# Moving one weight load in SyncE's queue: the gates' input weights behind the second group's first rows

## The chip, the cores and the metric

The kernel runs on one core of a Trainium2 chip. The metric is the device time of one execution in microseconds; the kernel before has a median of 2111.39 us over 7 runs (2110.67 to 2114.44). A core has TensorE (PE in the profile), VectorE (DVE), ScalarE (ACT), GpSimd (POOL) and SyncE (SP), each with its own list of instructions, and 16 DMA engines that serve the queues of all of them.

## The reference

The input `x` has 32 batches of 512 rows with 256 features, `adj` 32 masks of 512 by 512. A layer norm and a relu give `h`; one graph layer follows, and its result is added to `x`:

```python
h = relu(layernorm(x))
xc = transpose(h)                                     # features x rows
c = relu(bn1(conv1d(xc, conv1_w)))                    # kernel size 1
x_conv = relu(bn2(conv1d(c, conv2_w, pad=8)) + xc)    # kernel size 17, 256 to 256 channels
s = h @ w_se.T + b_se                                 # 3 features
A = exp(-|s_n - s_m|^2) * adj
x_nmp = A @ relu(h @ w_msg.T + b_msg)
gi = concat(x_conv, x_nmp) @ w_ih.T + b_ih            # 512 to 768: the gates' input weights
gh = h @ w_hh.T + b_hh                                # 256 to 768: the gates' hidden weights
r, z = sigmoid(gi_r + gh_r), sigmoid(gi_z + gh_z)
n = tanh(gi_n + r * gh_n)
out = x + (1 - z) * n + z * h
```

All is in 32-bit floats.

## The kernel before, in words

Features lie on partitions. The work is split into streams, Python generators that issue instructions, and a loop at the end of the kernel picks the next stream by a clock of its own: an estimate `now` of TensorE's time, to which every matmul adds its cost. The result is a fixed list of instructions for each engine; on the chip an engine goes through its list in order and waits on semaphores. The streams are:

- `begins` and `rows`: a batch's `h` is normalised, transposed to `hT` and stored in DRAM as `hd`. A row is conv1 of one batch: 8 matmuls `ps_g<-hT,w` of 512 columns, whose results ACT writes into `h1`, the input of the wide convolution.
- `conv`: the convolution of 17 taps, for seven groups of batches (`STARTS`, line 36: 116 columns, then 135 or 136), as 25 products a group, for which DVE makes the operands from `h1` and whose weights `w` are made once and then read back from DRAM (`w<-wd`). Its results go through `part` to DRAM as `cd`. A group's products can only begin when the rows of all its batches are in `h1`.
- `graphs`: messages, the kernel matrix, its mask (`m_sb`, read ahead four tiles at a time; for the first 8 batches TensorE transposes it) and the weighted sums, which go to DRAM as `nd`.
- `gates`: for each batch the products with `whh` (`ps_acc<-hTb,whh`) and with `wih` (`ps_acc<-xconv,wih` and `ps_acc<-xnb,wih`), the sigmoids, and the output. The stream starts when the pools of `late_pools` exist.

Loads go out from SyncE's queue, in the order in which the program issued them: SyncE issues one, waits where its buffer isn't free yet, and everything behind it waits too. Most stores go out from GpSimd's queue.

What lies around the change is the passage from the first group to the second. `late_pools` (line 819 on) is called by the convolution as soon as all 25 weights exist. It frees the memory in which the weights were made, puts there the pool `late`, and issues the loads of `whh` (768 KB, line 825) and `wih` (1536 KB, line 826). The rows of the second group, batches 4 to 8, come from `hd`: `load_row` (lines 207 to 212) reads one back into a tile `hT`, of which there are two. From batch 8 on (`TURNED`, line 40) `begin` lets DVE transpose the batch, also into a tile `hT`, and stores it from GpSimd's queue (line 942). So the load of batch 7's row takes over the tile from which batch 8 was stored, and waits until that store has landed:

```python
HR[b] = front.tile([P, ND, N], F32, name="hT", bufs=2)
nc.sync.dma_start(HR[b], HD[b])
```

A part of the program that is to be issued at a later point is handed to `later(t, f)` (line 158): it joins the list `LATER`, ordered by time, and is issued by `fill` once `now` has reached `t`, or by `settle`, which empties the list at some places.

Of the kernel before, what the change touches and what calls it, by code (L numbers as in the profile page):

```python
# [48 lines left out]
def kernel(  # L49
# [31 lines left out]
    nc = tc.nc  # L81
# [25 lines left out]
    now = 5.0  # L107
# [50 lines left out]
    def later(t, f):  # L158
        LATER.append((t, f))
        LATER.sort(key=lambda e: e[0])  # L160
# [576 lines left out]
    def convolution():  # L737
# [25 lines left out]
        for g in range(NG):  # L763
# [6 lines left out]
            for n in range(25):  # L770
# [7 lines left out]
                if late is None and len(WS) >= 25:  # L778
                    late_pools()
# [39 lines left out]
    def late_pools():  # L819
        nonlocal late, wih, whh  # L820
        prep_ctx.close()
        late = ctx.enter_context(tc.tile_pool(name="late", bufs=1))
        whh = late.tile([P, ND, 3 * D], F32, name="whh")
        wih = late.tile([P, 2 * ND, 3 * D], F32, name="wih")
        nc.sync.dma_start(whh, w_hh)
        nc.sync.dma_start(wih, w_ih)

    wih = whh = None

# [538 lines left out]
```

## Time and profile before

| | |
|---|---|
| median of 7 runs | 2111.39 us (2110.67 to 2114.44) |
| the profiled execution: time, span | 2113.81 us, 2111.8 us |
| TensorE busy | 2058.0 us |
| VectorE busy | 1512.6 us |
| ScalarE, GpSimd busy | 754.1 us, 338.9 us |
| DMA, mean over the span | 181 GB/s |
| load of `wih`: issued, time to landing | 216.9 us, 11.5 us |
| load of `whh`: issued, time to landing | 216.5 us, 6.8 us |
| first matmul with `whh`, with `wih` | 239.2 us, 269.0 us |

The span runs from the first to the last instruction of the program; times within it are counted from its start. PE is TensorE's matmuls, PEld its loads of weights, SPq the DMA issues of SyncE's queue. `hT<-hd` names what an instruction writes and what it reads. In a view of waits, a line gives who waited for whom, the sum in us, how often, and the longest. In a timeline, the first two numbers are start and duration in us, and the brackets hold the idle time before it and what ended it. q1 is the queue of SyncE's DMAs, q0 that of GpSimd's.

### The profile page before, as it was taken

How to read it: one execution, taken by the hardware profiler on the slowest of the kernel's cores; microseconds unless marked ns; L12 is line 12 of the kernel's file. 1: busy time of each engine (PE TensorE's matmuls, PEld its weight loads, DVE VectorE, ACT ScalarE, POOL GpSimd, SP SyncE). 2: the span in 40 equal slices, each digit the busy share in tenths (PEclk: the TensorE clock that was granted, in tenths of full speed). 3: DMA queues.
4: the chain of work that ended last, by engine and by line, in shares of the span. 5: the costliest groups of instructions: out<-in, count | busy, mean ns of one | idle time of the engine just before them, and what ended most of it. 6: DMA issues, size and time to landing. Idle time of an engine off the chain costs nothing.

```text
span 2111.8 us, 25916 instructions
## 1 busy us (share of the span) xinstructions
PE 2058.0 (97%) x8774; PEld 1259.3 (60%) x8774; DVE 1512.6 (72%) x2660; ACT 754.1 (36%) x1267; POOL 338.9 (16%) x582
## 2 busy tenths in 40 slices
PE   9999799999999999999999999999999999999998
PEld 6887466664666556665466565456664666654443
DVE  6887588985898668877488866588985877763333
ACT  5553533226432263232443322533224432233111
POOL 2000112221201021111121101211111110112111
PEclk9999999999999999999999999999999999999999
DMA  7445787776876777666776767677766655624332
GB/s 282 168 147 190 257 247 207 202 202 184 245 191 199 222 169 201 176 186 191 221 185 177 192 188 201 182 181 210 211 181 185 189 152 166 170 72 109 86 90 40
DMA packets 546436, 383.07 MB, mean 181 GB/s; under 512 B 456576, under 2 KB 473472, under 8 KB 545664
## 3 DMA queue, kind: packets, MB, share of 16 engines
q1 hardware_dynamic: 512992, 282.17, 50.5%
q0 software_dynamic: 28624, 86.01, 12.0%
q10 hardware_dynamic: 4688, 13.24, 1.6%
q8 instruction: 70, 1.15, 0.2%
q14 instruction: 62, 0.51, 0.1%
HBM read 281.95 MB, written 99.35 MB: 181 GB/s over the span
## 4 chain that ended last, share of the span: by engine, by line
PE 60%; issue 2%; DVE 2%; DMA 2%; POOL 1%; ACT 1%; SPq 0%; POOLq 0%; DVEq 0%
PE ps_acc L136 36%; PE ps_g L136 10%; PE ps_c L136 9%; PE ps_b L136 4%; DMA hT<-hd 1%; PE ps_b L867 1%; DVE y L127 1%; ACT r L127 0%; DMA hd<-hT 0%; PE ps_g L141 0%; DMA xnb<-nd 0%; SPq L339 0%; DVE r L127 0%; DVE z L127 0%; POOL out_dram L1078 0%
## 5 line engine op out<-in xcount | busy, mean ns | idle before, releaser
L136 PE MATMUL ps_acc<-hTb,whh 128*128 128x512 f32 x768 | 358.3, 598 | 18.6 <-ACT r L127 15.1
L136 PE MATMUL ps_acc<-xconv,wih 128*128 128x512 f32 (+1 forms) x772 | 362.6, 592 | 0.0
L136 PE MATMUL ps_acc<-xnb,wih 128*128 128x512 f32 (+1 forms) x772 | 358.7, 591 | 3.1 <-DMA xnb<-nd 3.0
L136 PEld LDWEIGHTS ps_c<-xd,w 128*128 128x128 f32 x2400 | 294.2, 191 | 31.8 <-issue 26.9
L136 PE MATMUL ps_c<-xd,w 128*128 128x135 f32 (+1 forms) x2400 | 303.5, 279 | 0.7 <-PE ps_g L141 0.7
L1078 POOL DMA_DIRECT2D out_dram<-res x252 | 164.0, 657 | 618.2 <-DVE res L127 538.2
L136 PEld LDWEIGHTS ps_acc<-hTb,whh 128*128 128x128 f32 x768 | 140.0, 190 | 179.3 <-issue 136.4
L136 PEld LDWEIGHTS ps_acc<-xnb,wih 128*128 128x128 f32 x772 | 142.7, 190 | 161.0 <-issue 153.3
L136 PEld LDWEIGHTS ps_acc<-xconv,wih 128*128 128x128 f32 x772 | 143.0, 190 | 157.4 <-issue 154.4
L136 PE MATMUL ps_g<-at,msg 128*128 128x512 f32 x512 | 227.2, 593 | 1.5 <-DVE at L127 1.5
L136 PEld LDWEIGHTS ps_b<-x,w 128*128 128x128 f32 x1200 | 157.2, 190 | 43.3 <-issue 37.0
L127 ACT ACTIVATE mid<-ps_b 128x270 f32<-128x270 f32 (+1 forms) x150 | 59.3, 396 | 345.4 <-PE ps_b L136 334.8
L127 DVE TENSOR_TENSOR r<-ps_acc,r 128x512 f32<-128x512 f32 (+1 forms) x65 | 44.2, 681 | 190.7 <-PE ps_acc L136 190.5
L136 PE MATMUL ps_b<-x,w 128*128 128x135 f32 (+1 forms) x1200 | 163.5, 279 | 0.7 <-ACT at L127 0.7
L136 PEld LDWEIGHTS ps_g<-at,msg 128*128 128x128 f32 x512 | 95.4, 190 | 112.4 <-issue 108.1
L127 DVE SCALAR_TENSOR_TENSOR x<-x,x 128x544 f32<-128x544 f32 (+5 forms) x161 | 137.7, 855 | 2.9
L136 PE MATMUL ps_g<-hT,w 128*128 128x512 f32 (+4 forms) x288 | 122.8, 573 | 15.1 <-DMA hT<-hd 11.2
L127 DVE TENSOR_TENSOR msg<-ps_g,bmsg 128x256 f32<-128x256 f32 x128 | 53.8, 421 | 109.0 <-PE ps_g L136 108.6
L127 ACT ACTIVATE z<-ps_acc,brz 128x512 f32<-128x512 f32 x64 | 44.0, 687 | 235.2 <-PE ps_acc L136 235.2
L127 DVE TENSOR_TENSOR x<-x 128x272 f32<-128x272 f32 (+5 forms) x280 | 127.6, 497 | 0.2
L136 PE MATMUL ps_g<-wmsg,hTg 128*128 128x259 f32 x496 | 124.1, 382 | 0.3 <-DVE aug L127 0.3
L127 DVE TENSOR_TENSOR xd<-x 128x544 f32<-128x544 f32 (+1 forms) x150 | 106.6, 718 | 24.0 <-PE ps_c L136 23.6
(121 smaller groups left out, 2591.2 us busy)
## 6 DMA issues: line engine op xcount, KB each, us to landing
w<-wd SPq DMA_DIRECT2D x125, 768.0 KB, 5.2
m_sb<-in_adj_dram SPq DMA_DIRECT2D x384, 64.0 KB, 3.2
hd<-hT POOLq DMA_DIRECT2D x32, 512.0 KB, 6.1
hT<-hd SPq DMA_DIRECT2D x32, 512.0 KB, 4.8
hTb<-hd SPq DMA_DIRECT2D x32, 512.0 KB, 5.4
xnb<-nd SPq DMA_DIRECT2D x64, 256.0 KB, 3.4
xconv<-cd SPq DMA_DIRECT2D x32, 512.0 KB, 5.5
res<-in_x_dram SPq DMA_DIRECT2D x256, 64.0 KB, 3.1
```

The costliest lines, as they stand in the source:

```text
L127: getattr(self.engine, name)(*tiles, **more)
L136: nc.tensor.matmul(ps, lhsT, rhs, **more)
L867: nc.tensor.matmul(pss[c], gr.left[k, :], gr.right[k, :], start=True, stop=True, tile_position=(32 * c, 0),)
L1078: queue.dma_start(OB[b][:, s.start // 32 : s.stop // 32, o * P + 32 * g : o * P + 32 * g + 32], y[at, s].rearrange("i (k j) -> i k j", j=32),)
```

## The change

The load of `wih` is no longer issued in `late_pools` at once but handed to `later`, for 14 us of the program's own clock after it.

```diff
         whh = late.tile([P, ND, 3 * D], F32, name="whh")
         wih = late.tile([P, 2 * ND, 3 * D], F32, name="wih")
         nc.sync.dma_start(whh, w_hh)
-        nc.sync.dma_start(wih, w_ih)
+        later(now + 14.0, lambda: nc.sync.dma_start(wih, w_ih))
```

In the instruction lists this moves one line of SyncE's. Before, its order was: `hTg` (batch 6), two `w`, `whh`, `wih`, `hT` (batch 7), `x_sb`, `w`, `hTb`, two `xnb`, `hT` (batch 8), four `m_sb`, `hTg` (batch 7), `xconv`. After, `wih` stands between the first and the second of the four `m_sb`. The lists of the other engines have the same instructions in the same order.

## The prediction

> **What bounds the kernel now.** I read the page's busy shares first, then who waited for whom around the point where the weights are fetched, then the timeline there, and last the DMA queues and the granted clock stage by stage.
>
> ```profile
> PE 2058.0 (97%) x8774; PEld 1259.3 (60%) x8774; DVE 1512.6 (72%) x2660; ACT 754.1 (36%) x1267; POOL 338.9 (16%) x582
> ```
>
> TensorE is busy for 2058.0 of 2111.8 us and its order is fixed, so only its idle time (53.8 us in all) and its clock can be won or lost. The waits of PE, and those of SyncE's queue, from 200 to 290 us:
>
> ```profile
> PE ps_g L136 <- DMA hT<-hd: 7.2, 1, 7.2
> ...
> SPq L211 <- DMA hd<-hT: 11.1, 1, 11.1
> ```
>
> The 7.2 us are PE's longest wait after the first load of weights, and it's one event: the second group's row of batch 7 waits for its `hT`. That load itself was held 11.1 us in SyncE's queue, until a store `hd<-hT` of GpSimd's had landed: the store of batch 8 reads the very buffer that the load overwrites. The timelines of PE, SyncE and GpSimd there (start, duration):
>
> ```profile
> 222.21 3.70 PE L136 MATMUL ps_g<-hT,w 128*128 128x512 f32 x8 [1.16 <-ACT at L127]
> 233.06 5.88 PE L136 MATMUL ps_g<-hT,w 128*128 128x512 f32 x8 [7.15 <-DMA hT<-hd]
> 239.21 1.88 PE L136 MATMUL ps_acc<-hTb,whh 128*128 128x512 f32 x4
> ...
> 216.49 0.37 SPq L825 DMA_DIRECT2D whh<-in_w_hh_dram  x1
> 216.92 0.58 SPq L826 DMA_DIRECT2D wih<-in_w_ih_dram  x1
> 228.66 0.33 SPq L211 DMA_DIRECT2D hT<-hd  x1
> ...
> 219.93 0.59 POOL L942 DMA_DIRECT2D hd<-hT  x1
> ```
>
> The store is issued at 219.93 and lands 8.7 us later, at 228.6; the load starts at 228.66, PE at 233.06. What held the store is seen in the DMA queues (two stretches: 219.9 to 222.7, and 223.7 to 228.1):
>
> ```profile
> DMA packets 236, 1.18 MB, mean 423 GB/s; under 512 B 21, under 2 KB 21, under 8 KB 231
> q1 hardware_dynamic: 236, 1.18, 104.9%
> ...
> DMA packets 249, 1.65 MB, mean 376 GB/s; under 512 B 29, under 2 KB 29, under 8 KB 157
> q1 hardware_dynamic: 108, 1.13, 65.1%
> q0 software_dynamic: 141, 0.52, 29.1%
> ```
>
> In the first stretch only SyncE's queue (q1) moves, at 423 GB/s. In the second the store (q0, all its 0.52 MB) shares the engines with 1.13 MB of q1, whose packets there are 12 KB each: that is `wih`, 1.57 MB in 128 rows, which takes 11.5 us from issue to landing. So `wih`, first used at 269.0, stands ahead of and beside a store that PE needs at 233. Last, the clock (PE busy, its loads, DVE, ACT, POOL, then PEclk, DMA share, GB/s):
>
> ```profile
> 227.26:230.67 3.41, 0.00 (x0) 0.00 (x0) 2.12 (x3) 0.37 (x2) 1.08 (x2) 1.00 0.48 126
> 230.67:234.08 3.41, 1.02 (x2) 0.54 (x3) 0.00 (x0) 0.00 (x0) 0.00 (x0) 0.50 0.97 295
> 234.08:237.50 3.42, 3.42 (x6) 1.35 (x5) 0.35 (x1) 0.65 (x2) 0.00 (x0) 0.50 1.04 418
> 237.50:240.90 3.40, 3.40 (x12) 1.66 (x11) 1.04 (x2) 3.40 (x8) 0.54 (x1) 1.00 1.04 390
> ```
>
> After the wait PE runs at half clock from 233.06 to 237.50: 4.44 us that do 2.22 us of work.
>
> [...] q1 and q0 at once, together 376 GB/s against 423 for q1 alone. [...] the store's first packet coming 3.8 us after its issue (at 223.7), while the same kind of store on an empty queue lands within 2.9 us. [...] its changes of clock lie on multiples of 3.41 us, and of the windows after the start those with at most 1.2 us of PE work are followed by half clock and those with 1.6 us or more are not.
>
> **The change, part by part.** No instruction is added or removed; the order of PE, DVE, ACT and GpSimd stays. One DMA issue of SyncE's, `wih` (one instruction, 0.58 us, 1.57 MB), moves past eight: `hT` of batch 7, `x_sb`, `w`, `hTb`, two `xnb`, `hT` of batch 8, and the first of four masks `m_sb`. That mask waits for PE's transposes (issued at 239.40 before), so `wih` goes out right after it.
>
> 1. *SyncE.* It gets 0.58 us back at 217, where it then waits until 228.6 anyway: nothing, the 11.1 us wait covers it; uncovered it would be 0.58 us.
>
> 2. *The store.* Up to its issue at 219.93 q1 had moved 1.24 MB. Of hTg, two w and whh (three times 0.524 and 0.786, 2.36 MB) 1.11 MB remain; with its own 0.52 MB that is 1.64 MB, and at 400 GB/s 4.1 us. About 0.6 us passed between the last packet and landing before (228.0 to 228.6). So it lands near 224.6 if the engines stay full. If it starts only when `whh` is through (222.7) and then needs the 1.8 us that an undisturbed store takes from first packet to landing, 224.5; if its first packet stays at 223.7, 225.5. Other stores of this form that had 0.67 to 0.89 MB of q1 beside them took 5.1 to 5.8 us, so 226 is the late end. I take 224.8, 3.8 us earlier than 228.6; ends 2.6 and 4.2.
>
> 3. *The load and PE's wait.* `hT` is then issued at 224.86; with the 4.26 us it took before, PE begins at 229.25 instead of 233.06. ACT evacuated the rows before it by 227.6, so no other wait ends later. The wait falls from 7.15 to about 3.3 us: **-3.8 us**.
>
> 4. *The clock.* The wait of 3.3 us is still nearly a window long. Moving the windows over all positions, with half clock after one with under 1.4 us of work, I get a mean cost of about 2.7 us for the 7.15 us wait and 2.3 for 3.3 us, each anywhere from zero or 0.7 to 3.4. Against this execution (2.2) that is 0, against a typical one -0.4. I take **-0.4**; ends -2.2 and +1.2.
>
> 5. *Next on PE.* After this row come four transposes and `ps_acc<-hTb,whh` at 239.21. `hTb` landed at 238.3, with 0.9 us to spare. Its issue moves by the same 3.8 us, to land by about 234.5, a little earlier still if two stores of `w` (0.52 MB, issued at 229.08 after DVE's own work) fall behind it. At half clock PE gets there at 235.4: no wait. With the clock kept, it gets there at 233.1 and waits about a microsecond, which takes back part of step 4's best end. I count 0.
>
> 6. *Where wih now lies.* It is issued at about 235.5, behind `hT` of batch 8 in its own queue, and with 11.5 us lands at 247. Its first matmul, 269.0 before, would come at 265: 18 us of cover. Behind it in the queue are three masks for the next graph (used near 264) and `hTg`, held by PE until 254. Beside it are the `cd` stores (issued 241.8 to 243.9 before, landed by 248.8; the buffers are wanted again by ACT at 255, the data at 258.5) and `nd` stores. From 240 to 252 the engines moved some 220 GB/s of about 400, room for over 2 MB. So 0, where an uncovered `wih` would cost its 3.9 us of engine time.
>
> 7. *To the end.* PE is fed by DVE, whose chain of operands starts when these rows are through (it waits 7.07 us until 252.08), so it moves along. Everything after is the same order started earlier. I find nothing with a fixed time that would absorb it.
>
> Sum: -3.8 - 0.4 = -4.2 us, with ends of about -7 and 0. Against the profiled execution (2113.81, span 2111.8) that is 2109.6; it stands 2.4 us above the median of the seven runs (2111.39, from 2110.67 to 2114.44). From the median: **2107.2**.
>
> **The rivals.** (a) *The stall goes altogether*: the store slips in between `whh`'s packets, lands by 224.0, and the clock holds; PE saves 4.5 and 2.2 us less the wait for `hTb` of about 1: some 5.7 us, 2105.7. For it: the work in the windows around a gap of 2.5 us at 564 was enough to keep the clock. Against: the 3.8 us delay of the store's first packet, when q1 was full. (b) *Another wait takes its place*: the load of batch 7 is at the head of six others either way, and `hTb`, `w` or half clock ends last, so that only about 1 us is kept: 2110.4. For it: `hTb` had but 0.9 us to spare. Against: these loads wait for nothing but the queue and move along. (c) *Slower*: `wih` comes too late. Where it stands now, a wait of SyncE's ahead of it would hold it: `hT` of batch 8 or the mask. PE's order being fixed, all gates' matmuls queue behind the first one on `wih`. It would decide only from an issue after 253.5 (265 less 11.5), and to lose 4.2 us net of the gain the issue would have to lie near 262: 2116. Against: the mask's issue is released by the first transposes, before 236. (d) *Nothing happens*, since the store is slow by itself (`hd<-hT` takes 6.1 us in the median): it would land at 226, which is the late end of step 2, -2.6 us, 2108.8.
>
> **How the numbers follow.** About 0.2%, 4.2 us, is what a measurement of this kernel can tell from no change. Chances: the forecast with (d) 0.72, (a) 0.12, (b) 0.09, (c) and other losses 0.07. The forecast's own range is 2104.8 to 2109, and half of it lies beyond 0.2%; with (a) this makes faster 0.48, same 0.45, slower 0.07. The range goes to -7 us and just past no change: 2104.2 to 2111.6.
>
> **What would show it.** In the changed profile: `hd<-hT` issued at 219.9 and landing in about 5 us instead of 8.7; SyncE's L211 wait of 11.1 us down to some 7; `hT` issued near 225; PE's wait for it near 3.3 us; half clock still there for one or two windows; `ps_acc<-hTb,whh` starting near 235; `wih` issued near 235.5 and no PE wait on it. The prediction is wrong if the store still lands after 227, if PE waits for `hTb` or `wih` instead, or if the 4 us seen at 240 aren't there at 290 or at the end.

## The result, and the profile after

The changed kernel takes 2105.04 us in the median of 15 runs (2101.75 to 2109.24), against 2111.55 for the kernel before in 35 runs beside it (2107.67 to 2115.13). The ratio is 0.9969, with a 95% interval from 0.9962 to 0.9976: 6.5 us faster, by the interval 5.1 to 8.0. A second series of five runs (e6 below) gave 0.9965 [0.9953, 0.9978]. The forecast, 2107.2, named the right event; the gain is half as large again as the 4.2 us forecast. Two executions far slower than the rest, one of e1 and the profiled one of e4 (0.75 of full clock), do not enter the ratios.

The profiled execution of the kernel after took 2102.61 us, with a span of 2100.6. Its busy shares, from the page:

```profile
PE 2053.8 (98%) x8774; PEld 1258.0 (60%) x8774; DVE 1512.7 (72%) x2660; ACT 754.0 (36%) x1267; POOL 338.9 (16%) x582
```

TensorE's busy time fell by 4.2 us with the same 8774 instructions. That is clock, not work (the mean granted clock was 0.996, against 0.993 before), and it is more than the change can own: the two profiled executions differ by 11.2 us where the medians differ by 6.5. Some stretches of half clock stand in one execution alone: before at 29.3, 230.7 and 1039.6 us, after at 559.7; those before at 264.8, 490.1 and 1343.4 have their like after, at 255.9, 481.2 and 1334.5. Following PE instruction by instruction, the kernel before was already 1.7 us behind at 33 us, long ahead of the change (half clock from 29 to 33 us, which the other of the two executions lacks), and gained or lost 0.4 to 2.0 us at a handful of later places. So the passage around the change is read by itself, from the issue of the store `hd<-hT` to the first `ps_acc<-hTb,whh`. The waits of PE and of SyncE's queue there (us in total, times, longest), from 200 to 290 us:

```profile
SPq L211 <- DMA hd<-hT: 8.1, 1, 8.1
...
PE ps_g L136 <- DMA hT<-hd: 2.8, 1, 2.8
...
PE ps_acc L136 <- DMA hTb<-hd: 0.5, 1, 0.5
```

SyncE's 11.1 us are 8.1, PE's 7.2 are 2.8, and a line stands below it that was not there: PE now waits for `hTb` too. The timelines of PE, SyncE and GpSimd (start, duration, idle time before and what ended it):

```profile
220.42 3.70 PE L136 MATMUL ps_g<-hT,w 128*128 128x512 f32 x8 [1.16 <-ACT at L127]
226.90 3.67 PE L136 MATMUL ps_g<-hT,w 128*128 128x512 f32 x8 [2.78 <-DMA hT<-hd]
230.41 0.60 PE L141 MATMUL ps_g<-ident,m_sb 128*128 128x128 f32 x4
231.47 1.96 PE L136 MATMUL ps_acc<-hTb,whh 128*128 128x512 f32 x4 [0.46 <-DMA hTb<-hd]
...
214.70 0.37 SPq L825 DMA_DIRECT2D whh<-in_w_hh_dram  x1
223.25 0.32 SPq L211 DMA_DIRECT2D hT<-hd  x1
224.64 0.42 SPq L225 DMA_DIRECT2D hTb<-hd  x1
231.04 0.33 SPq L336 DMA_DIRECT2D m_sb<-in_adj_dram  x1
231.43 0.43 SPq L826 DMA_DIRECT2D wih<-in_w_ih_dram  x1
...
218.14 0.59 POOL L942 DMA_DIRECT2D hd<-hT  x1
```

The store is issued at 218.14 and landed before 223.25, when `hT` goes out (all of this execution lies some 1.8 us earlier than the one before). PE starts the row at 226.90 and runs it at full clock, 3.67 us instead of 5.88. What the DMA queues moved between the store's issue and its landing (packets, MB, share of the engines), first in the kernel before, then in the kernel after:

```profile
q1 hardware_dynamic: 386, 2.70, 78.7%
q0 software_dynamic: 144, 0.52, 14.7%
...
hd<-hT POOLq DMA_DIRECT2D x1, 512.0 KB, 8.7
```

```profile
q1 hardware_dynamic: 253, 1.16, 55.5%
q0 software_dynamic: 144, 0.52, 25.4%
...
hd<-hT POOLq DMA_DIRECT2D x1, 512.0 KB, 5.1
```

Before, the stretch held 2.69 MB of SyncE's queue up to the landing itself and lasted 8.7 us; now it holds 1.14 MB and lasts 5.1 us. The 1.57 MB of `wih` that went away are the difference.

From store to `ps_acc<-hTb,whh`, the passage took 19.28 us before (219.93 to 239.21) and 13.33 after (218.14 to 231.47): 5.95 us less. By pieces: the store's flight 8.67 to 5.05, 3.62 less; the load of `hT` 4.26 to 3.52, 0.74 less; from the row's start to the `hTb` matmul 6.15 to 4.57, 1.58 less, which is 2.20 us of half clock gone, less 0.62 by which the wait for `hTb` now delays the matmul (the view counts 0.46 of it as idle time). These 5.95 us lie inside the interval of 5.1 to 8.0. The shifts at other places are of the size by which two executions of the same kernel (this one and e6 below) differ too.

### The profile page after: what moved, and what is told of

It reads as the page before. It is cut to its first block, busy times and chain, and to the rows that moved or that the text cites. A ratio compares the mean times of both kernels' runs of the same rounds, so it can differ in the third digit from the quotient of the medians.

```text
span 2100.6 us, 25915 instructions
## 1 busy us (share of the span) xinstructions
PE 2053.8 (98%) x8774; PEld 1258.0 (60%) x8774; DVE 1512.7 (72%) x2660; ACT 754.0 (36%) x1267; POOL 338.9 (16%) x582
## 3 DMA queue, kind: packets, MB, share of 16 engines
q8 instruction: 70, 1.15, 0.2%
## 4 chain that ended last, share of the span: by engine, by line
PE 64%; DVE 1%; issue 1%; ACT 1%; DMA 1%; SPq 0%; POOL 0%; DVEq 0%; ACTq 0%; POOLq 0%
PE ps_acc L136 38%; PE ps_g L136 11%; PE ps_c L136 9%; PE ps_b L136 4%; PE ps_b L867 1%; ACT r L127 1%; DMA hT<-hd 0%; PE ps_g L141 0%; DVE y L127 0%; DVE r L127 0%; DMA hd<-hT 0%; ACT at L127 0%; DVE z L127 0%; DVE right L127 0%; DVE at L127 0%
## 5 line engine op out<-in xcount | busy, mean ns | idle before, releaser
L136 PE MATMUL ps_g<-hT,w 128*128 128x512 f32 (+4 forms) x288 | 118.0, 555 | 9.6 <-DMA hT<-hd 5.5
```

What stands on the lines that cost most here:

```text
L136: nc.tensor.matmul(ps, lhsT, rhs, **more)
```

## The experiments

The theory on trial (A): what counts is how many bytes of SyncE's queue move between the store's issue and its landing, and PE's row follows from that. Against it: the store is slow by itself, or by the width of its neighbour's packets; the gain comes from the clock; or another load ends last.

**e1_store_first.** The kernel before, with the store of batch 8 issued earlier on GpSimd, ahead of an instruction of the layer norm (`rstd`, line 279) that waits for DVE; `wih` stays where it was.

```diff
-            yield dve.free + 0.4
-            nc.gpsimd.dma_start(HD[b], HT[b])
+            if b == TURNED: nc.gpsimd.dma_start(HD[b], HT[b])
+            yield dve.free + 0.4; b == TURNED or nc.gpsimd.dma_start(HD[b], HT[b])
```

> The kernel before, with GpSimd's store of batch 8 put ahead of its rstd instruction, so that it is issued near 215.4 us instead of 219.9; wih stays where it was. Theory A (PE waits for a chain: the bytes ahead of and beside the store, the store's landing, then the bytes ahead of the row's load in the same queue): the store lands near 220.5, but the load then stands behind whh and wih in SyncE's queue and lands near 229.5 instead of 232.9; PE's wait is about 3.6 us instead of 7.2, the time about 2108. Rival B (only the store's landing counts): the load lands near 225, PE doesn't wait, the clock stays up, about 2102. Rival C (the store is no part of it; the engines' total load is): 2111.5.

Measured: 2109.55 against 2113.16, ratio 0.9986 [0.9979, 0.9992]. The time, 3.0 us less by the ratio, is as theory A expected; the way to it isn't. The store was issued at 216.12, some 4.3 us earlier in the program than before (up to here this execution runs 0.48 us behind the one before), but its first packet came only 4.43 us later, and it landed at 223.69, after 7.57 us, where 220.5 was expected. `hT` could then be issued early, but its data still stood behind `whh` and `wih` in SyncE's queue and landed at 231.04:

```profile
223.74 0.33 SPq L211 DMA_DIRECT2D hT<-hd  x1
...
231.18 5.37 PE L136 MATMUL ps_g<-hT,w 128*128 128x512 f32 x8 [4.79 <-DMA hT<-hd]
```

So an earlier store alone takes only part of the wait away: 7.15 to 4.79 us, since `wih` now delays the load directly (7.30 us from issue to landing instead of 4.26).

**e2_both.** The kernel after with the same early store.

> The kernel after, with the same early store. Theory A: the store lands near 220.5, the load is issued then, has only whh's rest ahead of it and lands near 225; PE's wait for the row goes from 2.8 us to under 0.5, the clock stays up, and hTb lands before PE gets to it. About 3 us under the kernel after: 2102 (2100.5 to 2104). Rival B (what comes next on PE, hTb or w, already sets the time): 2105, with PE waiting about 3 us more for hTb.

Measured: 2106.5, ratio 0.9966 [0.9954, 0.9978], or 7.2 us less. The further 3 us expected did not show, though the interval (4.7 to 9.7 us) just reaches that far; it is no better than the kernel after by itself, and the row's wait, expected under 0.5 us, is 2.97. Two lines of its DMA queues between the store's issue and its landing (216.0 to 223.6), and the row's wait in its timeline:

```profile
q1 hardware_dynamic: 461, 1.76, 70.5%
...
hd<-hT POOLq DMA_DIRECT2D x1, 512.0 KB, 7.6
```

```profile
229.22 3.67 PE L136 MATMUL ps_g<-hT,w 128*128 128x512 f32 x8 [2.97 <-DMA hT<-hd]
```

The store went out some 4.3 us earlier in the program than in the kernel after (this execution runs 2.1 us behind that one), yet it took 7.6 us, so that it landed only 1.7 us earlier; and the load of `hT` then took 5.4 us instead of 3.5, beside the rest of `whh`, which landed at 225.93. The row was no earlier. While the store was under way SyncE's queue moved 1.76 MB instead of 1.14, although only `hTg` and one `w` (1.05 MB) had been issued before it: some 0.7 MB that was issued after the store went ahead of it or beside it. And all DMA together was slow just after such an early issue. The same stretch of the program, in e2 and then in the kernel after (last two columns: DMA share, GB/s):

```profile
217.00:220.00 3.00, 2.51 (x23) 2.28 (x21) 1.94 (x9) 0.68 (x2) 0.74 (x1) 1.00 0.75 250
```

```profile
215.00:218.00 3.00, 2.39 (x22) 2.15 (x20) 1.83 (x8) 0.81 (x3) 0.86 (x1) 1.00 0.93 355
```

In e1 the same stretch shows 261 GB/s; in the kernel before and in the other runs without the early store (e3, e6, e7, e9, e10) it shows 345 to 373. Why the engines were slower was not found.

**e3_behind_row.** `wih` is issued right behind `hT` of batch 7, ahead of `hTb`.

```diff
-        nc.sync.dma_start(wih, w_ih)
+        UNSENT.append(lambda: nc.sync.dma_start(wih, w_ih))
...
-            nc.sync.dma_start(HR[b], HD[b])
+            nc.sync.dma_start(HR[b], HD[b]); b == 7 and UNSENT and UNSENT.pop()()
```

> wih is moved behind the row's load of batch 7 alone, ahead of x_sb, w, hTb, xnb and the row of batch 8. Theory A: the store and the row are as in the kernel after (store about 5 us, PE's wait for the row about 2.8 us), but hTb lands 3.9 us later, as long as wih's 1.57 MB take, and PE waits for it about 4 us instead of 0.5; the time is 3.5 us above the kernel after, about 2108.5. Rival B (it only matters that wih is behind the row): the same as the kernel after, 2105.

Measured: 2115.39, ratio 1.0008 [0.9999, 1.0016]. The store landed after 4.70 us and the row waited only 2.5 us, as in the kernel after, but the whole gain was gone again, where theory A had left some 3 us of it:

```profile
PE ps_acc L136 <- DMA hTb<-hd: 5.5, 1, 5.5
PE ps_g L136 <- DMA hT<-hd: 2.5, 1, 2.5
```

PE now stood 5.5 us (4 expected) for `hTb`, which took 11.4 us to land behind `wih`, and its four matmuls after that took 3.49 us, at half clock, instead of 1.96. A shorter row wait is therefore worth nothing unless `hTb` comes earlier as well: the edit gains because `wih` went behind *both*.

**e4_whh_too** and **e12_whh_look.** The kernel after, with `whh` moved back too, behind two `xnb`; e12 is one execution of the same kernel, for its profile.

```diff
-        nc.sync.dma_start(whh, w_hh)
+        later(now + 8.0, lambda: nc.sync.dma_start(whh, w_hh))
```

> The kernel after, with whh moved too, behind the second xnb. With wih and whh gone, 0.33 MB are left ahead of the store instead of 1.11 (after) and 2.69 (before). Theory A, by bytes: the store takes 3.3 to 3.6 us instead of 5.05, PE's wait for the row goes from 2.8 to about 1.2 us; but whh then lands near the time at which PE wants it with hTb, so that PE waits 1 to 1.5 us more there: the time is as of the kernel after, 2105, with the wait moved. Rival B (the store's start is delayed by a fixed time, not by what is ahead): store 5 us, the row's wait 2.8 us, and the time 1 to 2 us above the kernel after.

> whh and wih both moved, one look, for its profile. The measured time of this kernel was within 0.1% of the kernel before, so 6 us of the gain are gone. Theory A: the store lands in 3.3 to 3.6 us and PE's wait for the row is under 1.5 us, but PE waits 3 to 6 us for whh, which stands behind 2.6 MB, with half clock after it. Rival B: the store takes 5 us as before and the row is no earlier.

Measured: e4 2112.58, ratio 0.9995 [0.9987, 1.0003], no gain left, where the time of the kernel after was expected. In e12's profile, the queues between the store's issue and landing, and PE's wait:

```profile
q0 software_dynamic: 144, 0.52, 43.8%
q1 hardware_dynamic: 79, 0.26, 21.2%
...
hd<-hT POOLq DMA_DIRECT2D x1, 512.0 KB, 3.0
```

```profile
PE ps_acc L136 <- DMA whh<-in_w_hh_dram: 2.7, 1, 2.7
```

With next to nothing beside it (0.26 MB of SyncE's queue) the store takes 3.0 us, so it isn't slow by itself. But `whh` is wanted right after the row, and PE waits for it at the place where the kernel after waits for `hTb`, with half clock from 236.86 to 240.28, where four matmuls took 3.44 us instead of 1.96. (That PE did not wait for the row here is not the store's doing alone: the rows of batches 6 and 7 took 10.11 us together, part of it at half clock, where the kernel after has 3.70 and 3.67.)

**e5_own_tile.** The kernel after, where the row of batch 7 is read into a tile of another ring, so that it no longer waits for the store of batch 8.

```diff
-            HR[b] = front.tile([P, ND, N], F32, name="hT", bufs=2)
+            HR[b] = late.tile([P, ND, N], F32, name="xconv", bufs=2) if b == 7 else front.tile(...)
```

> The kernel after, with batch 7's row loaded into a tile of the late pool (one of the two xconv tiles, not yet in use) instead of the tile that batch 8 is stored from. The load then waits for no store: it is issued right behind whh, near 215 us instead of 223.3. Theory A (the store's landing is what holds the row, and whh's and the rest's bytes only 2.4 MB): the row lands near 223, before PE has finished the rows before it, PE's wait for it (2.8 us) is gone, hTb is there in time too (it waits for nothing but the queue), and the time is 3 to 4 us under the kernel after. Rival B (the weights w, hTb or DVE set the next step anyway): PE waits as long somewhere before 240 us, and the time is that of the kernel after within 1 us.

Measured: 2103.07, ratio 0.9961 [0.9947, 0.9974]. That is about 1 us under e6 beside it, not 3 to 4, and not resolved. The row's wait went, and the next ones show:

```profile
224.89 3.67 PE L136 MATMUL ps_g<-xconv,w 128*128 128x512 f32 x8 [0.28 <-DMA xconv<-hd]
228.40 0.60 PE L141 MATMUL ps_g<-ident,m_sb 128*128 128x128 f32 x4
229.83 1.96 PE L136 MATMUL ps_acc<-hTb,whh 128*128 128x512 f32 x4 [0.83 <-DMA hTb<-hd]
...
264.00 2.08 PE L136 MATMUL ps_c<-xd,w 128*128 128x135 f32 x16 [2.06 <-issue]
```

PE is ahead of its loads now: 0.83 us for `hTb`, and 2.06 us at 264, where DVE, on its way to the next operand, had waited 1.26 us for batch 9's `x_sb<-xd`.

**e6_after_again.** The kernel after, unchanged, beside e5, e7 and e8.

> The kernel after as it is, on the same chip as the other runs of this call. The prediction's sum gives 4.2 us under the kernel before, the first measurement 6.5. If the excess is the clock (kept in most executions after a wait of 2.8 us), the profile shows again no half clock between 224 and 240 us, and the difference is again 6 to 7 us. If the clock falls in two executions of three, as moving the windows over all positions gives for a wait of 2.8 us, half clock is likely to be seen and the difference is 4 to 5.5 us.

Measured: 2103.87 (2103.58 to 2104.56), ratio 0.9965. Its profile shows the clock in another place. PE's timeline, and the two windows at half clock with the one ahead of them (PE busy, its loads, DVE, ACT, POOL, granted clock, DMA share, GB/s):

```profile
222.51 10.13 PE L136 MATMUL ps_g<-hT,w 128*128 128x512 f32 x16 [1.15 <-ACT at L127]
232.47 0.60 PE L141 MATMUL ps_g<-ident,m_sb 128*128 128x128 f32 x4
234.07 1.96 PE L136 MATMUL ps_acc<-hTb,whh 128*128 128x512 f32 x4 [1.00 <-DMA hTb<-hd]
```

```profile
218.33:221.75 3.42, 2.29 (x19) 1.22 (x17) 1.75 (x6) 1.70 (x4) 1.60 (x2) 1.00 1.02 411
221.75:225.16 3.41, 2.65 (x3) 1.17 (x4) 3.34 (x5) 1.69 (x4) 0.00 (x0) 0.50 0.69 270
225.16:228.57 3.41, 3.41 (x5) 1.35 (x4) 3.41 (x4) 2.23 (x5) 0.00 (x0) 0.50 0.71 229
```

Here half clock fell before the wait. The rows of batches 6 and 7 took 10.13 us together, the data for batch 7 arrived meanwhile, and the wait for it is gone altogether; PE still ended up waiting 1.00 us for `hTb`. Store to `hTb` matmul: 13.84 us, against 13.33. Two windows at half clock cost almost nothing (0.51 us more), since the time they took was waiting time, and `hTb` ends last either way.

**e7_after_warm** and **e8_before_warm.** Transposes without use (22 on the kernel after, 50 on the kernel before) keep PE at work in the wait, to take the clock out of the comparison.

```diff
+            yield HR_AT[b]; keep_warm(22 if (g, b) == (1, 7) else 0)     # e8: 50
```

> The kernel after, with 22 transposes of the identity (some 2.4 us, into a PSUM tile that nobody reads) on PE between the rows of batches 6 and 7. They fill the wait, so that the clock can't fall there if transposes count as work. If the wait costs half clock in part of the executions, the time is 1 to 2 us under the kernel after; if the clock is kept anyhow, it's the same within 0.5 us.

> The kernel before, with 50 transposes of the identity (some 5.5 us) on PE between the rows of batches 6 and 7. The row still comes at 233, but after PE work. Theory A (half clock is a cost of its own, about 2.5 us of the kernel before): the row's 8 matmuls take 3.7 us instead of 5.9, and the time is 2 to 2.7 us under the kernel before. Rival B (transposes don't count for the clock, or the time is made up at hTb, which then is late): no change within 0.7 us.

Measured: e7 2108.45, ratio 0.9988 [0.9981, 0.9994], 4.6 us slower than the kernel after without them (e6, 2103.87); e8 2112.0, 1.001 [1.0001, 1.0019], by the ratio 2 us slower than the kernel before. Neither outcome expected came, for e7 or for e8: such work in the wait doesn't pay here. In e8's timeline:

```profile
227.32 5.62 PE L146 MATMUL ps_acc<-ident 128*128 128x128 f32 x50
232.78 3.60 PE L136 MATMUL ps_g<-hT,w 128*128 128x512 f32 x8
236.22 0.60 PE L141 MATMUL ps_g<-ident,m_sb 128*128 128x128 f32 x4
238.29 1.96 PE L136 MATMUL ps_acc<-hTb,whh 128*128 128x512 f32 x4 [1.47 <-DMA hTb<-hd]
```

The row runs at full clock (3.60 us, not 5.88), and PE then gives 1.47 us of that back waiting for `hTb`. By this one profile, keeping the clock in the row was worth 1.1 us in the kernel before: from store to `hTb` matmul 18.17 us instead of 19.28. The time of e8 doesn't show it. e7's own profile (its fastest execution) is locally like the kernel after, with 13.72 us. Where the time of e7 and e8 went was not seen; that the transposes run late, and delay the row, in executions whose clock falls before the wait, is the author's estimate and was not shown.

**e9_thin_rows.** The kernel before, with `wih` in four loads whose rows are 3 KB instead of 12.

```diff
-        nc.sync.dma_start(wih, w_ih)
+        for k in range(4): nc.sync.dma_start(wih[:, k], w_ih[:, k])
```

> The kernel before with wih in its old place, but loaded by four DMAs of 3 KB a row instead of one of 12 KB. Theory A [...]: the store, which lands 8.7 us after its issue before, lands about 2 us sooner, after 6.5 to 7 us. The row's load then still stands behind the rest of wih, since the bytes are the same, so that it lands 2 to 3 us sooner and PE waits 4.2 to 5.2 us instead of 7.2; the time is 1.5 to 3 us under the kernel before. Rival B (only the number of bytes ahead and beside counts, not the packets): the store lands after 8.5 us again, the time is that of the kernel before.

Measured: 2107.88, ratio 0.9993 [0.9986, 0.9999], or 1.5 us less (0.2 to 3.0): the lower end of what theory A of this run forecast. From the store's issue to its landing:

```profile
q1 hardware_dynamic: 790, 2.63, 84.5%
q0 software_dynamic: 144, 0.52, 15.3%
...
hd<-hT POOLq DMA_DIRECT2D x1, 512.0 KB, 8.3
```

Twice the packets (790 against 386 of about the same bytes), and the store takes 8.3 instead of 8.7 us, which is rival B's forecast. But the landing tells of the last packet only. Seven us after its issue 139 of the store's 144 packets had moved here, against 69 in the kernel before and 75 in e8, both with rows of 12 KB. So beside rows of 3 KB most of the store moved earlier; five late packets kept the landing where it was, and why they were late is not shown. That PE's wait for the row is only 3.12 us here is no measure of it either: half clock fell ahead of the wait, as in e6 (221.53 to 228.35; batch 6's row took 6.66 us instead of 3.70). That the landing goes by the bytes also where no row of 12 KB is among them is seen in e5 and e11 (2.03 and 2.40 MB, 7.30 and 7.90 us), in the table below.

**e10_wih_later.** The kernel after with `wih` later still, behind four masks instead of one.

```diff
-        later(now + 14.0, lambda: nc.sync.dma_start(wih, w_ih))
+        later(now + 30.0, lambda: nc.sync.dma_start(wih, w_ih))
```

> wih goes out still later, behind all four masks instead of the first. Theory A (from behind the row of batch 8 on, its place is free, as nobody waits for what it meets): as the kernel after within 0.7 us, 6 to 7 us under the kernel before; PE waits as there (2 to 3.3 us for the row or at half clock before it, 0.5 to 1.3 us for hTb), and wih lands near 246 to 248, 13 us before its first use. Rival B (in its new place wih delays the masks, the cd stores, which took 7 us there instead of 3.4 to 4.8, or the row of batch 8): 1 us or more faster than the kernel after.

Measured: 2106.95 against 2110.09, ratio 0.9981 [0.9974, 0.9989], which is 4.0 us by the ratio. The passage is as in the kernel after (`hT` waited for 2.1 us, `hTb` 1.2, store to `hTb` matmul 13.39 us), `wih` landed at 247.68, and PE never waited for it. So the place of `wih` isn't critical at this end, as far as the profile shows. It gained 2 us less than the kernel after, where the same or more was expected. The two were not run side by side, and their intervals touch ([0.9974, 0.9989] and [0.9962, 0.9976]); the difference has no cause in the profile and stays open.

**e11_row_tile_x_later.** e5, and batch 10's load of `x_sb` held back by 9 us of the program's clock, so that `hTb` and the rows are served first.

```diff
-            nc.sync.dma_start(XS[b][:, c : c + step], ...)
+            go = lambda c=c, xs=XS[b]: nc.sync.dma_start(xs[:, c : c + step], ...)
+            later(now + 9.0, go) if b == TURNED + 2 else go()
```

> The kernel with batch 7's row in its own tile, and batch 10's x_sb (0.52 MB, not used before 250 us) moved behind the two xnb. With the store off the path the next thing PE waited for was hTb (0.8 us), and then at 262 us for operands (2.1 us), behind DVE's wait for a batch read back (x_sb<-xd). Theory A: hTb lands 1.3 us sooner, its wait is gone, the wait at 262 us stays; 1 to 2 us under the kernel after. Rival B (the wait at 262 us takes it all back): as the kernel after within 1 us.

Measured: 2100.66 (2099.47 to 2104.17, five runs), ratio 0.9958 [0.9946, 0.9971], the lowest of all. Both waits are gone:

```profile
225.89 3.67 PE L136 MATMUL ps_g<-xconv,w 128*128 128x512 f32 x8
229.40 0.60 PE L141 MATMUL ps_g<-ident,m_sb 128*128 128x128 f32 x4
229.83 1.88 PE L136 MATMUL ps_acc<-hTb,whh 128*128 128x512 f32 x4
```

What is left is 0.57 us at 263.27. It is clearly faster than the kernel before; its interval overlaps those of e5 and of the kernel after ([0.9962, 0.9976]).

**The runs side by side.** The bytes of SyncE's queue that moved between the store's issue and its landing, and the time that it took:

| kernel | SyncE's MB beside the store | store, us |
|---|---|---|
| e12 (`whh`, `wih` later) | 0.24 | 2.97 |
| e10, e6, e7, e3 | 1.03 to 1.07 | 4.60, 4.88, 4.89, 4.70 |
| after | 1.14 | 5.05 |
| e5, e11 (batch 7's row ahead, in a tile of its own) | 2.03, 2.40 | 7.30, 7.90 |
| e9, e8, before (`wih` ahead) | 2.61, 2.65, 2.69 | 8.33, 8.54, 8.67 |
| e2, e1 (store issued early) | 1.76, 1.78 | 7.63, 7.57 |

Without the last row that is a line of (8.67 - 2.97) / (2.69 - 0.24) = 2.3 us per MB, or some 430 GB/s, close to the 423 at which SyncE's queue ran alone in the kernel before. It gives 7.2 and 8.0 us for e5 and e11, whose bytes are not those of `wih`, but only 6.5 and 6.6 for e2 and e1. It is also a line of this passage: elsewhere in the profile of the kernel before, stores of this form with 1.04 and 1.56 MB beside them (issued at 120.67 and 271.36) took 6.6 and 6.8 us, where it gives 4.8 and 6.0. More bytes can also pass because a store takes longer, so the line by itself doesn't say which is cause. That `wih` is the cause follows from the runs where only it moved: 8.67 us before, 5.05 after, 4.70 in e3, 4.60 in e10.

The end of the passage, store to `hTb` matmul: 19.28 us before, 18.17 and 18.21 in e8 and e9; 13.33 after, 13.84, 13.72, 13.39 in e6, e7, e10. Except in the kernel before itself, all of these end with PE waiting for `hTb`.

The passage can also be followed on PE's own list, which takes in the runs whose store moved: how much earlier than in the profile of the kernel before PE comes to the same instruction, from 219.9 to 245.1 us of that profile. Beside it stands the gain in time by the ratio, with its interval (us; e12 with e4's time):

| kernel | PE's lead over the passage | gain in time |
|---|---|---|
| e11 | 9.2 | 8.9 (6.1 to 11.4) |
| e5 | 8.0 | 8.2 (5.5 to 11.2) |
| e2 | 6.3 | 7.2 (4.7 to 9.7) |
| after | 5.9 | 6.5 (5.1 to 8.0) |
| e6 (the kernel after again) | 5.4 | 7.4 (4.6 to 9.9) |
| e10 | 5.8 | 4.0 (2.3 to 5.5) |
| e7 | 5.5 | 2.5 (1.3 to 4.0) |
| e1 | 2.9 | 3.0 (1.7 to 4.4) |
| e12, e4 | 2.2 | 1.1 (-0.6 to 2.7) |
| e9 | 1.0 | 1.5 (0.2 to 3.0) |
| e8 | 1.0 | -2.1 (-4.0 to -0.2) |
| e3 | -0.5 | -1.7 (-3.4 to 0.2) |

In nine of the twelve, one execution's passage accounts for the gain within its interval. The others are e10 by a little, and the two with idle transposes, e7 and e8, which are slower than their passage says.

## Why the prediction was right, and where its sizes were off

**Step 1** (SyncE's 0.58 us cost nothing) held: SyncE still waits 8.1 us there.

**Step 2** (the store 3.8 us earlier, about 4.9 in flight) held: 5.05 us, 3.62 saved. Its way of counting, all of SyncE's remaining bytes plus the store's own at 400 GB/s, comes close to the line of the table. Rival (d), a store slow by itself, fell with e12: 3.0 us.

**Step 3** (PE's wait falls by the same 3.8, to 3.3 us) was a little short. The load of `hT` was priced at 4.26 us, from the kernel before; with `wih` out of its way it took 3.52. The wait fell to 2.78, by 4.4.

**Step 4** (the clock, -0.4) is the term that was mis-sized. Against the profiled execution the row ran 2.2 us faster, and by e8's profile keeping the clock was worth 1.1 even with `hTb` where it was. Two things made the difference, and the 1.4 us of PE work below which the step let the clock fall, its author's estimate, isn't one of them.

The first is luck. In each of the two profiled executions the changes of clock lie multiples of 3.413 us apart (to within 0.02), and these stretches are the windows meant here. A wait of 2.78 us, less than a window long, can fall within one window or across two. In the profiled execution of the kernel after it lay across two, of 2.34 and 1.70 us of work, and the clock was kept:

```profile
221.78:225.19 3.41, 2.34 (x6) 0.76 (x4) 3.41 (x3) 2.75 (x7) 0.00 (x0) 1.00 0.41 117
225.19:228.60 3.41, 1.70 (x4) 0.87 (x5) 2.40 (x3) 0.64 (x2) 1.08 (x2) 1.00 1.02 374
```

(The edges are counted from the execution's changes of clock, at 6.74 us and at 255.91, which lie 73 times 3.413 us apart.) By the step's estimate the clock would fall at about two positions of the window in three, as e6's expectation says. The second is that the step averaged over positions and priced half clock wherever it falls. When it falls before the wait, as in 4 of the 13 profiles read (batch 6's row took 5.08 us in e8 and 6.66 in e9 instead of 3.70, and the two rows 10.13 in e6 and 10.11 in e12), it fills the wait and costs next to nothing (e6: 0.5 us).

The prediction's reading of the trace needs one correction. Its limits, at most 1.2 us of PE work ahead of half clock and 1.6 or more otherwise, are right for the trace before only if the matmuls of line 867 are left out, whose form in the trace is `5*128` where the others have `128*128`; it doesn't say so. The window below, all of PE's work and then line 867 alone, held 1.88 us and was followed by half clock all the same; without line 867 it held 0.74:

```profile
261.40:264.81 3.41, 1.88 (x14) 1.05 (x15) 3.27 (x8) 3.41 (x7) 2.51 (x4) 1.00 1.03 236
```

```profile
261.40:264.81 3.41, 1.14 (x8) 0.31 (x8) 1.00 1.03 236
```

Counted like that, the profiles of the kernels before and after hold 1192 windows at full clock from 35 to 2090 us (595 and 597). Nine were followed by half clock: eight of these held at most 1.21 us of work, and one 1.70 (556.28 to 559.69, after). The other 1183 held 1.36 or more, and one of them, from 225.19 above, held 1.70 as well. So no single figure divides the two kinds, though 1.4 us would be wrong for only two of the 1192: the one of 1.70 and the one of 1.36. With line 867 counted in, four of the nine held 1.88 to 2.35 us, and the 1183 held 1.54 or more. The window ahead of e6's half clock held 2.29 us, 1.14 of them line 867, which leaves 1.15. That the matmuls of line 867 have no effect on the clock was not shown; no run varied them.

**Step 5** (`hTb`, counted 0, "about a microsecond" if the clock is kept) had the mechanism and the wrong weight. The clock was kept and PE waited 0.46, and 1.0 to 1.25 in e6, e7 and e10; so one of the prediction's own signs of being wrong, that PE waits for `hTb` instead, came true in small. In the kernel after `hTb` is what ends last, so the gain is set by how much earlier `hTb` lands, 4.3 to 6.0 us by the passage (18.17, taking e8 for the kernel before with its clock kept, less 13.84, up to 19.28 less 13.33), and not by the row. That is why the gain is near rival (a), 5.7 us, although the stall did not go altogether: 2.8 us of it remained, but half clock went. Rival (b), that only 1 us is kept, would need `hTb` to stay put, which is e3, where nothing was kept.

**Step 6** held: `wih` was issued at 231.43, landed at 241.06, and is first used at 261.01. The `cd` stores beside it grew from 3.4 to 4.8 us to about 7.0, and nobody waits for them; rival (c) is excluded, and e10 with `wih` landing 6.6 us later has no wait on it either.

**Step 7** (carried to the end) can't be seen in two profiles whose chance differences are of the same size, but the medians show no clear loss: 6.5 us (5.1 to 8.0) against the passage's 5.95.

## What to carry to other kernels

In this passage the store that frees a buffer landed 2.3 us later for each MB that SyncE's queue moved beside it; issuing it 4.3 us earlier, ahead of `whh`, did not free it of them (7.57 us in e1, 7.63 in e2). So order loads by when they are first used, and look for the big early one ahead of the small urgent one. A wait that is shortened is worth only what the next operand in the same queue allows: moving `wih` behind one of the two loads gained nothing (e3), behind both it gained 6.5 us, and moving `whh` as well gave it all back (e4). Price a half-clock stretch by what waits at its end, not by its length (e6's two windows cost 0.51 us), and don't fill a wait with idle work before that is known (e7 lost 4.6 us by it against e6, e8 2 us against the kernel before).

## What was unexpected of the hardware

- A store issued 4.3 us earlier from GpSimd's queue, just as SyncE's loads went out, took longer: first packet after 4.43 and 4.55 us, landing after 7.57 and 7.63 us (e1, e2), while all DMA together fell to 261 and 250 GB/s in a stretch where the runs without it had 345 to 373.
- The row width of the neighbour's transfer changed when most of a store moved, but hardly when it landed: after 7 us, 139 of 144 packets had moved beside rows of 3 KB (e9), 69 and 75 beside rows of 12 KB (before, e8), and it landed after 8.33 us against 8.67 and 8.54.
- With the matmuls of line 867 left out, eight of the nine windows that half clock followed in the profiles before and after held at most 1.21 us of PE work, and one 1.70; the other 1183 at full clock held 1.36 or more. Of the ten windows at half clock there, the nine that full clock followed held 3.13 us or more, and the one that half clock followed (from 230.67, before) 1.03; in e6 half clock went on after a window with 2.65. In 4 of 13 profiles (e6, e8, e9, e12) it came before the long wait and not after it.
